# Half a pair as the unit of work through matmul, scaling and multiplication, in a kernel of 496 pairwise products

## The chip, the core and the metric

The kernel runs on one core of a Trainium2 chip. The metric is the device time of one execution in microseconds (us). Medians are quoted; all runs told of here were in the fast state, and executions of one kernel agree within about 0.5% (0.8% in e10). A profile's span is about 2 us shorter than the device time. Ratios are computed as the mean time of one kernel's runs over that of the other's of the same rounds, so they are not quite the ratio of the medians quoted.

Engines: PE is TensorE (PEld its weight loads), DVE VectorE, ACT ScalarE, POOL GpSimd, SP the engine that issues the transfers here.

## The reference, cut to what matters

```python
# r_inputs (1024, 32, 128) float32, W (496, 128, 128) float32; I_IDX, J_IDX: all pairs i < j of 32 fields
v_i = inputs[:, I_IDX, :]
v_j = inputs[:, J_IDX, :]
transformed = jnp.einsum('bpd,ped->bpe', v_i, W)
return transformed * v_j                          # (1024, 496, 128): 260 MB of output
```

## The kernel before

For each pair q the output is a tile of 128 x 1024 float32 (two PSUM banks). The first 15 pairs are multiplied directly. In the other 481 the matmul works on split operands: each weight and field is cut by ScalarE and POOL into h, l and d. Two products (h with h, l with l) accumulate in PSUM, ScalarE multiplies the sum in place by 1 + EPS, a third product (d with d) is added on top, VectorE multiplies with the other field into an output tile, and SP stores it.

I call the first two products F and the third S. Between F and S of the same pair the scaling must run, so the source puts the S of an older pair there: it stands LAG pairs behind.

```python
LAG = 2
wpool = ctx.enter_context(tc.tile_pool(name="ws", bufs=3))
opool = ctx.enter_context(tc.tile_pool(name="o", bufs=6))
ppool = ctx.enter_context(tc.tile_pool(name="ps", bufs=4, space=bass.MemoryType.PSUM))   # tiles of 1024: 2 banks each
# ...
for q in range(NQ + LAG):
    if q < NQ:
        # ... every 4 pairs: load the weights of chunk c+3, split those of c+2; per field: load and split
        po[q] = ppool.tile([P, BT], F32, tag="po", name=f"po_{q}")
        # ...
                for t in (0, 1):                                  # F: four matmuls of 512 columns
                    for h in range(0, BT, HB):
                        nc.tensor.matmul(po[q][:, h : h + HB], w_s[c][t][:, r], x_s[i][t][:, h : h + HB],
                                         start=t == 0, stop=t == 1)
                nc.scalar.mul(po[q], po[q], 1.0 + EPS)            # scaling
    if q >= LAG:
        if q - LAG >= nq0:
            second(q - LAG)                                       # S: two matmuls
        finish(q - LAG)                                           # multiplication and store
```

(Calls reflowed, cuts marked with dots.) The framework in which the kernel is written sets all waits itself, and when it compiles it may also put the instructions of an engine into another order than the source has.

## Time and profile before

| | before |
|---|---|
| median of the runs beside the changed kernel | 897.93 us (896.86 to 898.89) |
| profiled span | 896.0 us |
| TensorE busy / DMA share of 16 engines | 85% / 92.3% |
| S waits for the scaling (PEld + PE) | 162.8 + 123.0 us |

How to read the group lines that the prediction shows: busy us in total, mean ns of one, then the engine's idle time before them and what ended most of it. A wait line has the waiting engine, line and tile, what it waited for, us in total, how often, and the longest.

### The profile page before, as it was taken

The numbers are of one execution on the slowest core, as the hardware profiler recorded it, in microseconds if no ns is written. First come the engines' busy times: TensorE is split into PE (matmuls) and PEld (weight loads), VectorE is DVE, ScalarE is ACT, GpSimd is POOL, SyncE is SP. The second block draws the span as 40 slices with busy tenths as digits, with TensorE's granted clock in tenths as the row PEclk, the third lists the DMA queues.
The fourth block names the chain that finished last, engine by engine and source line by source line (L and its number), as shares of the span: only waits on it lengthen the run. The fifth ranks groups of instructions, "written<-read, shape, count | busy, mean of one in ns | idle before, by whom it ended". The sixth has DMA issues, their size and how long they took to land.

```text
span 896.0 us, 10407 instructions
## 1 busy us (share of the span) xinstructions
PE 761.1 (85%) x2946; PEld 526.2 (59%) x2946; DVE 607.0 (68%) x498; ACT 558.2 (62%) x655; POOL 549.5 (61%) x523
## 2 busy tenths in 40 slices
PE   7988888888888888888888888888888888898887
PEld 2455555555666565555565666655656566665665
DVE  3666666666777666676676767776667777677766
ACT  2266666666676566566665667665756666666565
POOL 1878877777666774664747565665655647474441
PEclk9999999999999999999999999999999999999999
DMA  8999999899999898998998999998998899999997
GB/s 329 416 340 370 360 355 343 318 361 338 376 357 362 332 370 327 339 361 320 353 343 336 343 363 356 355 352 321 355 341 334 336 339 330 343 345 339 337 342 304
DMA packets 94666, 310.03 MB, mean 346 GB/s; under 512 B 10513, under 2 KB 10769, under 8 KB 94609
## 3 DMA queue, kind: packets, MB, share of 16 engines
q1 hardware_dynamic: 94608, 309.37, 92.3%
q8 instruction: 23, 0.38, 0.2%
q14 instruction: 35, 0.28, 0.1%
HBM read 49.28 MB, written 260.05 MB: 345 GB/s over the span
## 4 chain that ended last, share of the span: by engine, by line
PE 32%; ACT 25%; issue 19%; POOL 11%; DMA 1%; DVE 0%; POOLq 0%; ACTq 0%; DVEq 0%
ACT po L177 20%; PE po L170 17%; PE po L135 14%; ACT wh L86 4%; POOL wl L87 4%; POOL wd L89 4%; POOL whs L88 2%; DMA out_dram<-ot 1%; ACT xh L100 1%; POOL xls L101 1%; DVE ot L128 0%; POOL xl L102 0%; POOLq L87 0%; ACTq L177 0%; POOL xd L103 0%
## 5 line engine op out<-in xcount | busy, mean ns | idle before, releaser
L128 DVE TENSOR_TENSOR ot<-po,x 128x1024 f32<-128x1024 f32 (+1 forms) x498 | 607.0, 1220 | 285.4 <-ACT po L177 141.7
L177 ACT ACTIVATE po<-po 128x1024 f32<-128x1024 f32 x481 | 476.9, 1009 | 298.5 <-PE po L170 298.5
L135 PE MATMUL po<-xd,wd 128*128 128x512 f32 x962 | 325.7, 420 | 123.8 <-ACT po L177 123.0
L87 POOL TENSOR_TENSOR wl<-w,wh 128x512 fp32r<-128x512 f32 x121 | 154.5, 1277 | 301.7 <-ACT wh L86 301.7
L135 PEld LDWEIGHTS po<-xd,wd 128*128 128x128 f32 x962 | 152.7, 188 | 257.5 <-ACT po L177 162.8
L170 PE MATMUL po<-xh,wh 128*128 128x512 f32 x962 | 300.9, 394 | 0.0
L170 PE MATMUL po<-xl,wl 128*128 128x512 f32 x962 | 298.1, 391 | 0.0
L170 PEld LDWEIGHTS po<-xl,wl 128*128 128x128 f32 x962 | 180.6, 188 | 42.2
L170 PEld LDWEIGHTS po<-xh,wh 128*128 128x128 f32 x962 | 180.6, 188 | 42.1 <-issue 0.5
L89 POOL TENSOR_TENSOR wd<-wl,whs 128x512 fp32r<-128x512 f32 x121 | 156.6, 1294 | 7.9
L86 ACT ACTIVATE wh<-w 128x512 fp32r<-128x512 f32 x121 | 75.5, 624 | 19.3 <-DMA w<-in_wt_dram 19.3
L88 POOL TENSOR_SCALAR whs<-wh 128x512 f32<-128x512 f32 x121 | 75.1, 621 | 10.2
L101 POOL TENSOR_TENSOR xls<-x,xh 128x512 f32<-128x512 f32 x52 | 67.4, 1296 | 4.2
L103 POOL TENSOR_TENSOR xd<-xh,xl 128x512 fp32r<-128x512 f32 x52 | 66.9, 1287 | 2.2
L100 ACT ACTIVATE xh<-x 128x512 fp32r<-128x512 f32 x52 | 32.1, 621 | 13.6 <-PE po L170 8.7
L102 POOL TENSOR_SCALAR xl<-xls 128x512 fp32r<-128x512 f32 x52 | 32.4, 623 | 4.4
L159 PE MATMUL po<-x,w 128*128 128x512 f32 x60 | 29.6, 656 | 6.2 <-DMA x<-in_xt_dram 6.2
L159 PEld LDWEIGHTS po<-x,w 128*128 128x128 f32 x60 | 12.3, 209 | 22.6 <-issue 21.6
L86 ACT ACT_TABLE_LOAD x1 | 1.3, 1283 | 0.7 <-PEq L196 0.7
L196 POOL MEMSET const-float32-0.0<- 128x1 f32 x1 | 0.1, 99 | 0.2 <-issue 0.2
L196 POOL MEMSET const-bfloat16-1.0<- 128x1 bf16 x1 | 0.1, 102 | 0.0
L196 POOL MEMSET const-uint8-127<- 128x1 uint8 x1 | 0.1, 102 | 0.0
(1 smaller groups left out, 0.1 us busy)
## 6 DMA issues: line engine op xcount, KB each, us to landing
out_dram<-ot SPq DMA_DIRECT2D x494, 512.0 KB, 3.8
w<-in_wt_dram SPq DMA_DIRECT2D x123, 256.0 KB, 3.9
x<-in_xt_dram SPq DMA_DIRECT2D x30, 512.0 KB, 6.0
x<-in_xt_dram SPq DMA_DIRECT2D x4, 256.0 KB, 4.4
out_dram<-ot SPq DMA_DIRECT2D x4, 256.0 KB, 2.6
w<-in_wt_dram SPq DMA_DIRECT2D x1, 192.0 KB, 2.6
w<-in_wt_dram SPq DMA_DIRECT2D x1, 64.0 KB, 1.8
```

Source lines behind the costliest of these rows:

```text
L86: nc.scalar.mul(h, raw, 1.0 - 2.0**-13)
L87: nc.gpsimd.tensor_tensor(l, raw, h.bitcast(F32), ALU.subtract)
L88: nc.gpsimd.tensor_scalar(hs, h.bitcast(F32), EPS, 1.0, ALU.mult, ALU.mult)
L89: nc.gpsimd.tensor_tensor(d, l.bitcast(F32), hs, ALU.subtract)
L100: nc.scalar.mul(h[:, s], x_sb[f][:, s], 1.0 - 2.0**-13)
L101: nc.gpsimd.tensor_tensor(ls, x_sb[f][:, s], h[:, s].bitcast(F32), ALU.subtract)
L103: nc.gpsimd.tensor_tensor(d[:, s], h[:, s].bitcast(F32), l[:, s].bitcast(F32), ALU.subtract)
L128: nc.vector.tensor_tensor(ot[:, s], po[q][:, s], x_sb[j][:, s], ALU.mult)
L135: nc.tensor.matmul(po[q][:, h : h + HB], w_s[q // WC][2][:, r], x_s[i][2][:, h : h + HB], start=False, stop=True, skip_group_check=True,)
L159: nc.tensor.matmul(po[q][:, h : h + HB], w_raw[c][:, q % WC, :], x_sb[i][:, h : h + HB], start=True, stop=True,)
L170: nc.tensor.matmul(po[q][:, h : h + HB], w_s[c][t][:, r], x_s[i][t][:, h : h + HB], start=t == 0, stop=t == 1,)
L177: nc.scalar.mul(po[q], po[q], 1.0 + EPS)
```

## The change

Its intent: a unit is half a pair, so that each PSUM bank goes round by itself. A unit's bank is scaled, finished and freed sooner, eight banks replace four pairs of banks, and S follows three units behind. The store is still one per pair. Loads of the first two fields are issued from ScalarE.

```diff
-LAG = 2
+LAG = 3
-    ppool = ctx.enter_context(tc.tile_pool(name="ps", bufs=4, space=bass.MemoryType.PSUM))
+    ppool = ctx.enter_context(tc.tile_pool(name="ps", bufs=8, space=bass.MemoryType.PSUM))
-    load_x(NF - 2, 2)
-    load_x(NF - 1, 2)
+    load_x(NF - 2, 2, nc.scalar)
+    load_x(NF - 1, 2, nc.scalar)
...
+    def first(u):
+        q, h = divmod(u, 2)
...
+        po[u] = ppool.tile([P, HB], F32, tag="po", name=f"po_{u}")
...
+            for t in (0, 1):
+                nc.tensor.matmul(po[u], w_s[c][t][:, r], x_s[i][t][:, s], start=t == 0, stop=t == 1)
+            nc.scalar.mul(po[u], po[u], 1.0 + EPS)
+
+    def second(u):
...
+            nc.tensor.matmul(
+                po[u], w_s[q // WC][2][:, r], x_s[i][2][:, s], start=False, stop=True, skip_group_check=True
+            )
...
+        nc.vector.tensor_tensor(ots[q][:, s], po.pop(u), x_sb[j][:, s], ALU.mult)
...
+    for u in range(2 * NQ + LAG):
...
+            first(u)
+        if u >= LAG:
+            second(u - LAG)
```

More of the change, by code (lines that the diff above doesn't have):

```diff
@@ L61, with load_x @@
     opool = ctx.enter_context(tc.tile_pool(name="o", bufs=6))
-    ppool = ctx.enter_context(tc.tile_pool(name="ps", bufs=4, space=bass.MemoryType.PSUM))
+    ppool = ctx.enter_context(tc.tile_pool(name="ps", bufs=8, space=bass.MemoryType.PSUM))
     x_sb = {}
-    def load_x(f, pieces=1):
+    def load_x(f, pieces=1, eng=None):
         x_sb[f] = xpool.tile([P, BT], F32, tag=f"x{f}", name=f"x_{f}")
@@ L69, in load_x @@
         for k in range(pieces):
-            nc.sync.dma_start(out=x_sb[f][:, k * s : (k + 1) * s], in_=xt[:, f, k * s : (k + 1) * s])
+            (eng or nc.sync).dma_start(out=x_sb[f][:, k * s : (k + 1) * s], in_=xt[:, f, k * s : (k + 1) * s])
     w_raw = {}
@@ L116 @@
     load_w(2)
-    out_v = out.rearrange("q e b -> q e b")
-    po = {}
-    def finish(q):
-        j = pairs[q][1]
-        ot = opool.tile([P, BT], F32, tag="ot", name=f"ot_{q}")
-        pieces = 2 if q >= NQ - 2 else 1
-        s0 = BT // pieces
-        for k in range(pieces):
-            s = slice(k * s0, (k + 1) * s0)
-            nc.vector.tensor_tensor(ot[:, s], po[q][:, s], x_sb[j][:, s], ALU.mult)
-            nc.sync.dma_start(out=out_v[q, :, s], in_=ot[:, s])
-    def second(q):
-        i, _ = pairs[q]
-        r = slice(q % WC * P, (q % WC + 1) * P)
-        for h in range(0, BT, HB):
+    po, ots = {}, {}
@@ new lines, in first @@
+    def first(u):
+        q, h = divmod(u, 2)
+        i, c = pairs[q][0], q // WC
+        r = slice(q % WC * P, (q % WC + 1) * P)
+        s = slice(h * HB, (h + 1) * HB)
+        po[u] = ppool.tile([P, HB], F32, tag="po", name=f"po_{u}")
+        if q < nq0:
+            nc.tensor.matmul(po[u], w_raw[c][:, q % WC, :], x_sb[i][:, s], start=True, stop=True)
+        else:
+            for t in (0, 1):
+                nc.tensor.matmul(po[u], w_s[c][t][:, r], x_s[i][t][:, s], start=t == 0, stop=t == 1)
+            nc.scalar.mul(po[u], po[u], 1.0 + EPS)
@@ L135, in second @@
+    def second(u):
+        q, h = divmod(u, 2)
+        i, j = pairs[q]
+        r = slice(q % WC * P, (q % WC + 1) * P)
+        s = slice(h * HB, (h + 1) * HB)
+        if q >= nq0:
             nc.tensor.matmul(
-                po[q][:, h : h + HB], w_s[q // WC][2][:, r], x_s[i][2][:, h : h + HB], start=False, stop=True,
-                skip_group_check=True,
-            )
-    for q in range(NQ + LAG):
-        if q < NQ:
+                po[u], w_s[q // WC][2][:, r], x_s[i][2][:, s], start=False, stop=True, skip_group_check=True
+            )
+        if h == 0:
+            ots[q] = opool.tile([P, BT], F32, tag="ot", name=f"ot_{q}")
+        nc.vector.tensor_tensor(ots[q][:, s], po.pop(u), x_sb[j][:, s], ALU.mult)
+        if q >= NQ - 2:
+            nc.sync.dma_start(out=out[q, :, s], in_=ots[q][:, s])
+        elif h == 1:
+            nc.sync.dma_start(out=out[q], in_=ots[q])
@@ L142 @@
+    for u in range(2 * NQ + LAG):
+        if u < 2 * NQ:
+            q = u // 2
             i, j = pairs[q]
             c = q // WC
-            if q % WC == 0:
+            if u % (2 * WC) == 0:
                 if c + 3 < nchunk:
                     load_w(c + 3)
-                for k in ([c + 2] if c > 0 else [0, 1, 2]):
+                for k in [c + 2] if c > 0 else [0, 1, 2]:
                     if c0 <= k < nchunk:
                         split_w(k)
-            if j == i + 1:
-                for f in ([i - 4] if i < NF - 2 else [NF - 6]):
-                    if f >= 0:
-                        load_x(f)
+            if u % 2 == 0 and j == i + 1:
+                f = i - 4 if i < NF - 2 else NF - 6
+                if f >= 0:
+                    load_x(f)
@@ L154 @@
                 if 0 <= i - 1 < NF - 1 - NATIVE:
                     split_x(i - 1)
-            po[q] = ppool.tile([P, BT], F32, tag="po", name=f"po_{q}")
-            if q < nq0:
-                for h in range(0, BT, HB):
-                    nc.tensor.matmul(
-                        po[q][:, h : h + HB],
-                        w_raw[c][:, q % WC, :],
-                        x_sb[i][:, h : h + HB],
-                        start=True,
-                        stop=True,
-                    )
-            else:
-                r = slice(q % WC * P, (q % WC + 1) * P)
-                for t in (0, 1):
-                    for h in range(0, BT, HB):
-                        nc.tensor.matmul(
-                            po[q][:, h : h + HB],
-                            w_s[c][t][:, r],
-                            x_s[i][t][:, h : h + HB],
-                            start=t == 0,
-                            stop=t == 1,
-                        )
-                nc.scalar.mul(po[q], po[q], 1.0 + EPS)
@@ L178 @@
-        if q >= LAG:
-            if q - LAG >= nq0:
-                second(q - LAG)
-            finish(q - LAG)
+            first(u)
+        if u >= LAG:
+            second(u - LAG)
 def kernel(**inputs):
```

## The prediction

> **What bounds the kernel now.** I read the page first (busy shares, DMA queue, groups), then the waits, then the order of TensorE's work in the middle of the run, then DMA over short windows.
>
> ```profile
> PE 761.1 (85%) x2946; PEld 526.2 (59%) x2946; DVE 607.0 (68%) x498; ACT 558.2 (62%) x655; POOL 549.5 (61%) x523
> DMA packets 94666, 310.03 MB, mean 346 GB/s; under 512 B 10513, under 2 KB 10769, under 8 KB 94609
> q1 hardware_dynamic: 94608, 309.37, 92.3%
> L128 DVE TENSOR_TENSOR ot<-po,x 128x1024 f32<-128x1024 f32 (+1 forms) x498 | 607.0, 1220 | 285.4 <-ACT po L177 141.7
> L177 ACT ACTIVATE po<-po 128x1024 f32<-128x1024 f32 x481 | 476.9, 1009 | 298.5 <-PE po L170 298.5
> ```
>
> No vector engine is near full: DVE, ACT and POOL each lie idle about a third of the time. TensorE shows 85%, but that is modelled. The DMA engines show 92% at a mean of 346 GB/s. So two candidates remain: TensorE with gaps, and the DMA. The waits say where TensorE stops:
>
> ```profile
> PEld po L135 <- ACT po L177: 162.8, 195, 1.7
> DVE ot L128 <- ACT po L177: 141.7, 89, 1.6
> PE po L135 <- ACT po L177: 123.0, 245, 1.2
> ```
>
> The third product (L135) waits 245 times for ScalarE's scaling (L177). Nothing waits for an output transfer here, so the DMA isn't a wait yet. In TensorE's own order of time (start us, length, count, idle before):
>
> ```profile
> 455.58 0.73 PE L135 MATMUL po<-xd,wd 128*128 128x512 f32 x2 [0.69 <-ACT po L177]
> 456.14 0.63 PE L170 MATMUL po<-xh,wh 128*128 128x512 f32 x2
> ...
> 457.07 0.62 PE L170 MATMUL po<-xh,wh 128*128 128x512 f32 x2
> 457.53 0.61 PE L170 MATMUL po<-xl,wl 128*128 128x512 f32 x2
> 458.43 0.70 PE L135 MATMUL po<-xd,wd 128*128 128x512 f32 x2 [0.28 <-ACT po L177]
> 458.96 0.63 PE L170 MATMUL po<-xh,wh 128*128 128x512 f32 x2
> ...
> 459.89 0.62 PE L135 MATMUL po<-xd,wd 128*128 128x512 f32 x2
> 460.35 0.62 PE L170 MATMUL po<-xh,wh 128*128 128x512 f32 x2
> ...
> 461.27 0.63 PE L135 MATMUL po<-xd,wd 128*128 128x512 f32 x2
> 462.60 0.73 PE L135 MATMUL po<-xd,wd 128*128 128x512 f32 x2 [0.69 <-ACT po L177]
> ```
>
> Call the first two products of a pair F (four matmuls) and the third S (two). The source says F S F S with S two pairs behind. What stands here is S, F F S F S F S, S: two S and two F adjoin, and S follows its own F by one pair, or by none (the S at 462.60 belongs to the F at 460.35). The program was reordered when it was compiled. Undisturbed, S plus F takes 461.27 - 459.89 = 1.38 us. Four pairs take 462.60 - 455.58 = 7.02 us instead of 4 x 1.38 = 5.52. The lost 1.50 us: 0.44 before 458.43, 0.87 before 462.60 (1.33 instead of 0.46), the rest in S pairs that start 0.1 us slower. Over 481 pairs, 481/4 x 1.50 = 180 us. **TensorE's gaps behind the scaling are the bound**, and the DMA stands close behind:
>
> ```profile
> 24.00:28.00 4.00, 4.00 (x11) 1.80 (x10) 3.02 (x3) 0.00 (x0) 3.76 (x5) 1.00 1.04 420
> 28.00:32.00 4.00, 4.00 (x11) 1.81 (x10) 2.93 (x3) 0.63 (x1) 3.83 (x5) 1.00 1.02 416
> 440.00:445.00 5.00, 3.62 (x15) 2.37 (x15) 2.06 (x2) 2.77 (x3) 2.77 (x3) 1.00 0.99 376
> 445.00:450.00 5.00, 4.28 (x19) 3.15 (x18) 4.29 (x4) 2.62 (x4) 2.16 (x3) 1.00 0.72 266
> 450.00:455.00 5.00, 4.61 (x19) 3.06 (x18) 3.07 (x4) 3.86 (x5) 1.34 (x2) 1.00 0.85 329
> ```
>
> The last two columns are DMA share and GB/s. Fed without a break (the first 40 us) the engines move 416 to 422 GB/s; in the middle they get 266 to 376, because outputs arrive unevenly. So the 92% isn't saturation[...].
>
> **What the Trainium skill says.** "PSUM — Partial Sum Buffer", Terms and "The four PSUM rules": a matmul's output lies in one bank of 512 float32, there are eight, and two engines may not be in one bank at once. A pair of 1024 columns is two banks, so four pair buffers are all of PSUM and so are eight half buffers; the change adds no memory, it frees each bank sooner. "Perfetto Trace Analysis", "Identifying Performance Opportunities": a consistent bubble can mean too few buffers for the next tile; the pattern that repeats every four pairs agrees. The same page, "Optimizing Scalar/DVE Operations": an instruction on PSUM carries about 51 ns on ScalarE and 125 ns on VectorE, and profiled latency hides an overlap. The trace: two scalings back to back last 1.93 us though one lasts 1.01, so the pitch is 0.92; the four half-wide multiplications at the end last 685 ns each, two of them 1.29 together, a pitch of 0.61. "DMA: Bandwidth & Descriptors", "Issuing engines are not separate DMA queues": another issuing engine saves issue time only; no run before shows loads from ScalarE.
>
> **The change part by part.**
> 1. TensorE: same matmuls, same weight loads (2946 each): 481 x 1.38 = 664 us, with no gain or loss from the halves.
> 2. ScalarE: 962 scalings of 512 instead of 481 of 1024. A half's pitch is an estimate, half of 0.92 plus half the skill's 51 ns, 0.49 us; 962 x 0.49 = 471 instead of 481 x 0.92 = 443. With 173 splits at about 0.53: 563 us. It costs 28 us, beside other work.
> 3. VectorE: 992 halves at 0.61 to 0.685 are 605 to 680 us instead of 607. Its pitch per pair, 1.22 to 1.37, stays just under TensorE's 1.38. Not on the path, but with little left.
> 4. The PSUM loop, in source order. Before: F 0.92, two further S and F 2.76, S 0.46, handover 0.2, multiplication 1.22: 5.56 us until the bank is free, against the 5.52 in which four buffers come round. No slack, so any split of 0.62 us on ScalarE breaks the order into what we saw. After: F 0.46, three units 2.07, S 0.23, handover 0.2, multiplication 0.69: 3.65 against the same 5.52, so 1.87 us of slack. This is the gain.
> 5. The lag: between an F and its S now lie 3 x 0.69 = 2.07 us; handover 0.2 plus a scaling of about 0.6 plus a split of 0.54 ahead of it is 1.34. It fits. So the 180 us can go: 896 - 180 = 716 us if TensorE alone set the end.
> 6. Loads of the first two fields from ScalarE: TensorE waits 6.2 us for x before 9.91 us. They share bandwidth with the loads they now overlap, so I count 1 us of gain.
> 7. DMA: same bytes, 310.03 MB. At 1.38 us per pair the store alone is 0.524 MB / 1.38 = 380 GB/s, the weights 0.262 MB per four pairs another 47, the fields about 17 MB over 664 us another 20 (with the first ones, which came earlier): near 445, above the 416 to 422 that it reached. So **the DMA becomes the bound before TensorE does**. Floor: 310.03 MB / 0.416 = 745 us, plus about 4 us of start and tail: 749. Over the whole run in windows of 4 us, the 44 windows with a DMA share of at least 1.02 moved 403 GB/s on average: 310.03 / 0.403 = 769, plus 4: 773. I add 7 us for the early fields, where POOL's split of a field (two halves of 1.30 + 0.62 + 1.29 us, 6.4 us) comes every 6 to 10 pairs, and for leftover gaps: 780. The runs' median lies 2 us above the profiled span, hence **782 us**.
>
> **The rivals.**
> (a) The order stays broken. The new order is also made when compiling, and it broke before at the start of each group of four pairs, where the split weights come due. If what broke it is POOL or ScalarE and not PSUM, TensorE still drains there: one scaling of 0.6 us and handovers, about 0.9 us per four pairs, 120 x 0.9 = 108 us over 715: 820 to 830. For it: the alignment with the four pairs. Against: POOL is 61% busy and waits 302 us for the weights' first split.
> (b) TensorE's floor is reached because stores pack better than I think: 716 to 745. Against: no stretch above 422 GB/s.
> (c) VectorE becomes the bound. If a half costs its full 685 ns plus the 0.16 us seen between multiplications, 0.845 x 992 = 838 us, about 850 in all. Against: that 0.16 is TensorE's pace showing, since queued halves took 0.61.
> (d) The saturated DMA with mostly stores does only 360, as some windows at full share did (356 at a share of 1.0): 861 us and no gain over 5%. Against: the stretches over 410 directly after a backlog.
>
> **Range and chances.** The central case is DMA at 403 GB/s; its floor at 416 gives 749, and with an even flow perhaps 752. Upwards (a), and parts of (c) and (d), reach 820 to 850. Range 752 to 835. Within 2% means above 880, which needs (d) or a badly broken order together with more; slower needs a new stall bigger than the old.
>
> **What would show it.** Right: L135's waits for L177 fall from 123 us to below 30; TensorE shows source order; the mean rate rises to about 395 GB/s, with most slices over 390; VectorE, or the output's issue, now waits for landed outputs. Step 2 is checked by the scaling's mean (near 580 ns), step 3 by 685 ns. Wrong: L135 still waiting for scalings by the hundred (a); VectorE above 90% (c); DMA share at 1.0 with 360 GB/s (d); a rate above 425 (b).

## The result, and the profile after

The changed kernel takes **931.2 us** (930.87 to 931.59, 4 runs) against 897.93: ratio 1.0371, 95% interval 1.0353 to 1.0389. It is slower; the range of the prediction ended at 835.

From the page of the changed kernel: busy shares, what the DMA moved, the two groups.

```profile
PE 856.3 (92%) x2946; PEld 500.4 (54%) x2946; DVE 676.1 (73%) x992; ACT 628.8 (68%) x1136; POOL 549.3 (59%) x523
DMA packets 94676, 310.12 MB, mean 334 GB/s; under 512 B 10512, under 2 KB 10768, under 8 KB 94608
L145 DVE TENSOR_TENSOR ot<-po,x 128x512 f32<-128x512 f32 x992 | 676.1, 691 | 250.4 <-PE po L140 230.1
L132 ACT ACTIVATE po<-po 128x512 f32<-128x512 f32 x962 | 548.6, 582 | 273.9 <-PE po L131 245.9
```

TensorE's 92% instead of 85% isn't more work: in the order of time below a matmul is recorded as 0.39 us long though the next begins 0.23 us after it (458.62, 458.85), so a stop of up to 0.16 us leaves no gap in the record. Weight loads, of which there are as many as before, went from 526.2 to 500.4 us busy. The DMA is less used than before (334 against 346 GB/s). The waits of the third product, now line 140, for the scaling, now line 132:

```profile
PEld po L140 <- ACT po L132: 263.0, 703, 1.0
ACT po L132 <- PE po L131: 245.9, 355, 5.3
PE po L140 <- ACT po L132: 42.6, 146, 0.6
```

The prediction wanted 123 us to fall below 30. Both kinds together went from 285.8 us in 440 waits to 305.6 us in 849. TensorE's order of time shows where (F is lines L131, S is L140; start us, length, count):

```profile
456.44 0.47 PE L140 MATMUL po<-xd,wd 128*128 128x512 f32 x1 [0.30 <-ACT po L132]
...
458.05 0.50 PE L140 MATMUL po<-xd,wd 128*128 128x512 f32 x1
458.38 0.40 PE L131 MATMUL po<-xh,wh 128*128 128x512 f32 x1
458.62 0.39 PE L131 MATMUL po<-xl,wl 128*128 128x512 f32 x1
458.85 0.39 PE L140 MATMUL po<-xd,wd 128*128 128x512 f32 x1
...
459.69 0.49 PE L140 MATMUL po<-xd,wd 128*128 128x512 f32 x1
...
461.41 1.10 PE L140 MATMUL po<-xd,wd 128*128 128x512 f32 x2
462.35 0.39 PE L131 MATMUL po<-xh,wh 128*128 128x512 f32 x1
...
463.74 0.47 PE L140 MATMUL po<-xd,wd 128*128 128x512 f32 x1 [0.30 <-ACT po L132]
```

The same pattern as before stands here, with halves: F F S F S F S ... S S over eight units, then again. From 456.44 to 463.74 are 7.30 us for four pairs; before it was 7.02. Over 120 such groups that is 0.28 x 120 = 34 us, less 2.9 us that the start gained (the first split product begins at 32.3 us instead of 35.2): 31, and the spans differ by 33.5. So the loss is in the pattern, all along the run (7.30 and 7.02 are also the medians over all groups of the two traces).

Is the lag of three units there? The listing of the compiled program gives each engine's instructions in their final order. This is TensorE's in the changed kernel; the number after po is the unit (48 rows per eight pairs, cut):

```
L131 Matmult po_488 <- xh, wh_61     L131 Matmult po_488 <- xl, wl_61
L131 Matmult po_489 <- xh, wh_61     L131 Matmult po_489 <- xl, wl_61
L140 Matmult po_488 <- xd, wd_61
L131 Matmult po_490 <- xh, wh_61     L131 Matmult po_490 <- xl, wl_61
L140 Matmult po_489 <- xd, wd_61
...
L140 Matmult po_494 <- xd, wd_61
L140 Matmult po_495 <- xd, wd_61
L131 Matmult po_496 <- xh, wh_62     (the next group of four pairs)
```

It isn't. S(488) stands one unit behind F(488), and S(495) directly behind S(494), with no F after its own. Counted over each compiled program, how many F start between an F and its S:

| program | LAG in the source | 0 | 1 | 2 | 3 |
|---|---|---|---|---|---|
| before (pairs) | 2 | 125 | 356 | 0 | |
| changed (halves) | 3 | 130 | 828 | 1 | 3 |
| changed, LAG 1 (built, not run) | 1 | 131 | 826 | 5 | 0 |
| changed, LAG 5 (built, not run) | 5 | 130 | 830 | 1 | 1 |

Counted from the order of TensorE's instructions in the traces, the first two rows come out the same. The lag in the source made next to no difference to the compiled program. A lag of one *pair* had become a lag of one *half*.

### The profile page after: what moved, and what is told of

It reads as the page before. It is cut to its first block, busy times and chain, and to the rows that moved or that the text cites. A ratio compares the mean times of both kernels' runs of the same rounds, so it can differ in the third digit from the quotient of the medians.

```text
span 929.5 us, 11870 instructions
## 1 busy us (share of the span) xinstructions
PE 856.3 (92%) x2946; PEld 500.4 (54%) x2946; DVE 676.1 (73%) x992; ACT 628.8 (68%) x1136; POOL 549.3 (59%) x523
## 2 busy tenths in 40 slices
DMA packets 94676, 310.12 MB, mean 334 GB/s; under 512 B 10512, under 2 KB 10768, under 8 KB 94608
## 4 chain that ended last, share of the span: by engine, by line
PE 58%; ACT 16%; POOL 15%; issue 8%; DMA 2%; DVE 0%; POOLq 0%; SPq 0%; ACTq 0%; DVEq 0%
PE po L131 30%; PE po L140 26%; ACT po L132 14%; POOL xls L101 5%; POOL xd L103 4%; POOL wd L89 2%; POOL xl L102 2%; DMA out_dram<-ot 2%; PE po L128 2%; POOL wl L87 1%; POOL whs L88 1%; ACT xh L100 1%; ACT wh L86 1%; DVE ot L145 0%; DMA x<-in_xt_dram 0%
## 5 line engine op out<-in xcount | busy, mean ns | idle before, releaser
L145 DVE TENSOR_TENSOR ot<-po,x 128x512 f32<-128x512 f32 x992 | 676.1, 691 | 250.4 <-PE po L140 230.1
L132 ACT ACTIVATE po<-po 128x512 f32<-128x512 f32 x962 | 548.6, 582 | 273.9 <-PE po L131 245.9
L140 PE MATMUL po<-xd,wd 128*128 128x512 f32 x962 | 440.1, 458 | 65.5 <-ACT po L132 42.6
L131 PE MATMUL po<-xl,wl 128*128 128x512 f32 x962 | 379.6, 395 | 0.0
L131 PE MATMUL po<-xh,wh 128*128 128x512 f32 x962 | 379.2, 394 | 0.0
L140 PEld LDWEIGHTS po<-xd,wd 128*128 128x128 f32 x962 | 179.2, 186 | 351.3 <-ACT po L132 263.0
L131 PEld LDWEIGHTS po<-xl,wl 128*128 128x128 f32 x962 | 180.5, 188 | 41.9 <-POOL wl L87 0.2
L131 PEld LDWEIGHTS po<-xh,wh 128*128 128x128 f32 x962 | 181.3, 189 | 11.8 <-issue 0.2
L102 POOL TENSOR_SCALAR xl<-xls 128x512 fp32r<-128x512 f32 x52 | 32.3, 622 | 4.4
```

Of the source, the lines that this page charges most:

```text
L102: nc.gpsimd.tensor_scalar(l[:, s], ls, 1.0 / EPS, 1.0, ALU.mult, ALU.mult)
L131: nc.tensor.matmul(po[u], w_s[c][t][:, r], x_s[i][t][:, s], start=t == 0, stop=t == 1)
L132: nc.scalar.mul(po[u], po[u], 1.0 + EPS)
L140: nc.tensor.matmul(po[u], w_s[q // WC][2][:, r], x_s[i][2][:, s], start=False, stop=True, skip_group_check=True)
L145: nc.vector.tensor_tensor(ots[q][:, s], po.pop(u), x_sb[j][:, s], ALU.mult)
```

## The experiments

Theory 1: the compiled order took the lag away, and TensorE stops behind the scaling as before, only twice as often. Theory 2: halves cost more in themselves (fixed parts of the doubled instructions on ScalarE and VectorE, twice the handovers). A third question was the prediction's: where the DMA binds.

The first tool is a call of the framework that pins an instruction behind the one that stands before it on the same engine in the source. It adds no wait for completion.

### e1, e2, e3, e4

e1 and e2, the change and the kernel before with TensorE held in source order (all matmul calls alike):

```diff
-                nc.tensor.matmul(po[u], w_s[c][t][:, r], x_s[i][t][:, s], start=t == 0, stop=t == 1)
+                tc.keep_in_program_order(nc.tensor.matmul(po[u], w_s[c][t][:, r], x_s[i][t][:, s], start=t == 0, stop=t == 1))
```

> The changed kernel with TensorE's matmuls held in source order, so that the third product stands three units behind in the compiled program too (in the changed kernel as compiled it stands one unit behind in 828 of 962 cases and none in 130). Theory 1 (the compiled order took the lag away, TensorE stops behind the scaling): the waits of the third product for the scaling fall from about 306 us together to under 40, and the time falls from 931 to 760 to 810, where the output transfers bind. Theory 2 (halves cost more in themselves: fixed parts of the doubled number of instructions on ScalarE and VectorE and twice the handovers): stays above 890.

> The kernel before, whole pairs, with TensorE's matmuls held in source order (third product two pairs behind; compiled as it was, one behind in 356 of 481 cases and none in 125). Theory 1: faster as well, 770 to 830; if the four pair buffers are as tight as the prediction says (5.56 us against 5.52), it lies 10 to 40 us above e1. Theory 2: about 20 us under e1 or more, and both near their unheld times (898 and 931).

e3 is e1 with a lag of one:

```diff
-LAG = 3
+LAG = 1
```

> As e1 with a lag of one unit in the source. Theory 1: between an F and its S lies 0.69 us (one S, one F) where the handovers and a half's scaling need about 0.86, so each unit takes about 0.82 instead of 0.69: 962 x 0.82 = 789, plus 41 of start and end: 830 to 850; the rest up to 931 is then the emptying at each group of four pairs. Theory 2: near 931.

e4 is the changed kernel, not held, with half the bytes stored:

```diff
-            nc.sync.dma_start(out=out[q], in_=ots[q])
+            nc.sync.dma_start(out=out[q, :, :HB], in_=ots[q][:, :HB])
```

> The changed kernel with only the first half of each output stored (wrong result on purpose, 130 MB less; the compiled order then is the source's, three units behind in 959 of 962 cases, without being held). Theory 1: the transfers are out of the way, TensorE alone sets the end: 700 to 730. Theory 2: above 850, since the halves' costs are all still there.

Measured (ratios to the kernel before in the same rounds):

| run | what | lag compiled | us | ratio (95%) |
|---|---|---|---|---|
| e1 | halves, held | 3 | 776.88 | 0.866 (0.865 to 0.868) |
| e2 | pairs, held | 2 | 781.46 | 0.871 (0.870 to 0.873) |
| e3 | halves, held, LAG 1 | 1 | 860.73 | 0.960 (0.958 to 0.962) |
| e4 | halves, half of each output stored (wrong result) | 3 | 712.57 | 0.795 (0.793 to 0.796) |

Theory 1 holds: the same instructions in source order take 777 instead of 931, and the kernel before gains as well, 781 instead of 898. It is TensorE's order that differs: ScalarE's weight split stands behind the sixth scaling of a group both in the changed kernel's trace and in e1's, all 121 times. Theory 2 falls: e1 has all of the halves' costs, and its list has one wait of an S for the scaling, of 0.4 us. One expectation was missed: e2 lies 5 us above e1, not 10 to 40. So with the order held, the change itself is worth 0.6%. Lines of e1's page and waits:

```profile
PE 726.2 (94%) x2946; PEld 542.3 (70%) x2946; DVE 638.2 (82%) x992; ACT 624.1 (81%) x1136; POOL 549.7 (71%) x523
DMA packets 94676, 310.12 MB, mean 400 GB/s; under 512 B 10512, under 2 KB 10768, under 8 KB 94608
PEld po L131 <- DVE ot L145: 86.5, 137, 1.9
DVE ot L145 <- DMA out_dram<-ot: 41.0, 51, 1.9
```

Here the rate is 400 GB/s over the whole span, VectorE waits for output tiles still on their way to memory, and TensorE's F in turn waits for VectorE. The transfers bind e1, as the prediction had expected of the change.

e3 separates two parts of the loss. With a lag of one throughout and no emptying at each group it takes 861, and its S wait for the scaling again:

```profile
PEld po L140 <- ACT po L132: 206.4, 657, 0.6
```

Against e4's 713, where TensorE alone sets the end, that is 148 us over 962 units, 0.154 us each. I had expected 830 to 850: 0.82 us per unit was a little low. The rest, 931 - 861 = 70 us or 0.58 per group of four pairs, I put down to the emptying. That is not shown by itself: in e3 ScalarE's weight split stands behind the last scaling of a group and not behind the sixth, and e9 below shows that its place alone can be worth 26 us.

The lag's arithmetic can be read from the changed kernel's order of time above: the second matmul of an F begins at 458.62 and the next instruction could begin at 458.85; its S begins at 459.69. These 0.84 us are the scaling (0.58) with its handovers (0.26). A lag of one half covers S and F of halves, 0.69 us, so the S at 459.69 stops for 0.15; the next instruction starts another 0.1 late, and these 0.25 us let the next S pass without a stop. So every second S stops: 458.05 to 459.69 are 1.64 us for two units where two undisturbed ones take 1.38. Before, with a lag of one pair, the S at 458.43 belongs to the F at 456.14, which is through at 457.07: the scaling (1.01) and its handovers (0.35) took 1.36 us, and S and F of a pair cover 1.38. The cover was halved by the change; the thing to be covered wasn't.

### e5, e6, e7, e8: pairs against halves, and how much lag

e5 is e2 with half of each output stored:

```diff
-            nc.sync.dma_start(out=out_v[q, :, s], in_=ot[:, s])
+            nc.sync.dma_start(out=out_v[q, :, k * s0 : k * s0 + s0 // 2], in_=ot[:, k * s0 : k * s0 + s0 // 2])
```

> As e2 (whole pairs, TensorE in source order), with half of each output stored (wrong result on purpose). It asks what the halves are worth when the transfers are out of the way; e4, the same with halves, took 713. If the four pair buffers bind (in e2 the weight loads of F wait 432 times for the multiplication, 134 us): a pair stays at about 1.50 us, 481 x 1.50 + 41 = 763, so 750 to 775. If in e2 the transfers were the bound and the buffers only passed that on: 710 to 725.

e6 is e2 with LAG = 1; e7 and e8 are e1 with LAG = 2 and LAG = 5.

> As e2 with a lag of one pair in the source. Between an F and its S then lie S and F of whole pairs, 1.39 us, where the scaling with its handovers needs about 1.26: only the pairs with a split of 0.54 us ahead stop, about 0.4 us per four pairs, 49 us over a TensorE floor of 705, so the transfers still bind: 770 to 790, while the same lag of one with halves (e3) took 861. If a lag of one hurts whole pairs as it hurts halves: 840 to 870.

> As e1 with a lag of two units: 1.39 us between an F and its S against about 0.86 needed, 1.40 with a split ahead. Theory 1: nothing left to wait for, 772 to 785, as e1 (777). If the lag matters in proportion to its number: halfway to e3, about 815.

> As e1 with a lag of five units. The way round a bank grows by two units to 3.65 + 1.38 = 5.03 us against 5.52, still inside. If the transfers bind: 772 to 785 again. If the looser lag helps further: under 765; if the banks become tight: over 790.

| run | what | us | ratio (95%) |
|---|---|---|---|
| e5 | pairs, held, LAG 2, half of each output stored (wrong result) | 778.75 | 0.868 (0.867 to 0.870) |
| e6 | pairs, held, LAG 1 | 781.13 | 0.871 (0.869 to 0.873) |
| e7 | halves, held, LAG 2 | 778.69 | 0.869 (0.866 to 0.871) |
| e8 | halves, held, LAG 5 | 777.68 | 0.867 (0.865 to 0.869) |

e5 shows what the change set out to cure. With 130 MB less to store, pairs stay at 779 (expected 750 to 775 if the buffers bind, so 4 us over) while halves (e4) reach 713. The wait line of e5, and its order of time:

```profile
PEld po L170 <- DVE ot L128: 137.5, 429, 2.3
```

```profile
456.95 0.73 PE L170 MATMUL po<-xh,wh 128*128 128x512 f32 x2
...
459.99 0.73 PE L170 MATMUL po<-xh,wh 128*128 128x512 f32 x2
...
463.02 0.73 PE L170 MATMUL po<-xh,wh 128*128 128x512 f32 x2
```

F waits for the multiplication that frees its buffer, 429 times, once for nearly every pair. The F at 463.02 takes the buffer of the one at 456.95, four pairs earlier: 6.07 us for four pairs, 1.52 each. So four pair buffers at a lag of two hold TensorE at 1.52 us per pair where it could do 1.38, and eight halves at a lag of three lift that: 66 us, but only where neither the order nor the transfers are in the way. How much of the 66 us needs halves is open, because e4 also has the shorter lag (three halves are 2.07 us, two pairs 2.76). e2's 781 comes from this round of the buffers (its same wait is 134.1 us, 432 times), e1's 777 from the transfers; that they come out so near to each other is chance.

e6 shows that a lag of one doesn't hurt pairs: 781, where it costs halves 861. The shorter lag also shortens the round of the buffers (that wait falls to 41.1 us, 80 times), and the transfers bind at 398 GB/s. Between its waits for the transfers e6 runs at 1.38 us per pair (S begin at 457.53, 458.90, 460.28 and 461.67), where e5's pairs take 1.38 and 1.65 in turn, so a shorter lag is a rival to halves here; pairs at a lag of one with half of each output stored were not run. e7 and e8 show that with halves a lag of two or five does as well as three: 1.38 us of cover is enough for 0.84.

### e9 to e12: is there a part of the transfers in it, and a better version

e9 is e3 with half of each output stored (the diff of e4). e10 gives each half its own output tile and store:

```diff
-    opool = ctx.enter_context(tc.tile_pool(name="o", bufs=6))
+    opool = ctx.enter_context(tc.tile_pool(name="o", bufs=12))
...
+        ot = opool.tile([P, HB], F32, tag="ot", name=f"ot_{u}")
+        nc.vector.tensor_tensor(ot, po.pop(u), x_sb[j][:, s], ALU.mult)
+        nc.sync.dma_start(out=out[q, :, s], in_=ot)
```

> As e3 (halves, held in source order, a lag of one unit: 861), with half of each output stored (wrong result on purpose). If TensorE's stop behind the scaling is all that binds at this lag: 845 to 862. If the transfers had a part in e3's time, as the drop from e1 to e4 (777 to 713) might suggest: under 820.

> As e1 with an output tile and a store for each half (12 tiles of 512 instead of 6 of 1024; the same bytes, rows of 2 KB instead of 4 KB). An attempt at a better version: e1 moves 400 GB/s on average and its VectorE waits 41 us for output tiles. If finer tiles keep the transfers better fed: 755 to 770. If the engines' rate is all there is: 774 to 785; if shorter rows cost rate: over 790.

e9 took 887.08 us (ratio 0.989), *more* than e3, and missed both of its expectations. In its compiled program ScalarE's weight split stands one unit earlier, ahead of the last scaling of a group instead of behind it; ScalarE had not been held. e11 and e12 hold it too, with full and with half stores:

```diff
-        nc.scalar.mul(h, raw, 1.0 - 2.0**-13)
+        tc.keep_in_program_order(nc.scalar.mul(h, raw, 1.0 - 2.0**-13))
```

(and likewise the field's split and the scaling).

> e3 again (halves, a lag of one unit, full stores), now with ScalarE's instructions in source order too. e9 came out 26 us slower than e3 although it stores half, and in its compiled program ScalarE's splits stand at other places. With both held, e11 and e12 have the same order on both engines. If TensorE's stop behind ScalarE is all that binds at this lag: e11 and e12 within 10 us of each other, both between 850 and 900.

> e9 again with ScalarE's instructions in source order too: within 10 us of e11 if the transfers have no part at a lag of one; 25 us or more above e11 (as e9 over e3) if e9's delay came from something else than ScalarE's order; 25 us or more below if the transfers do bind in e11.

e11 took 861.18 us (0.961), e12 858.42 (0.958). So at a lag of one the transfers have next to no part, and e9's 26 us came with ScalarE's order. The changed kernel as compiled moves 334 GB/s, fewer than e11's 361, so I take the transfers to be out of its loss as well, though no run stored half in exactly its order.

e10 took 824.49 us (0.920), worse than e1's 777, as the last of its expectations had it. Its page (with a granted TensorE clock of 0.974, and a DMA share of 101.7%):

```profile
DMA packets 165823, 310.24 MB, mean 378 GB/s; under 512 B 18416, under 2 KB 18672, under 8 KB 165744
```

The same bytes in 165,823 packets instead of 94,676 moved at 378 instead of 400 GB/s. There are also twice as many stores, so whether the shorter rows or their number cost it is not separated. e1, the change with TensorE held in source order, is the fastest: correct, and 13.4% less time than the kernel before. e7 and e8 are equal to it within the noise, and pairs held in order (e2, e6) come within 1%.

### What moved the order

Compiling again with less stored, and counting as above (built; of these only the first and the last row were run, as the changed kernel and e4, and their traces give the same counts):

| stored of each output | 0 | 1 | 2 | 3 |
|---|---|---|---|---|
| all | 130 | 828 | 1 | 3 |
| 7/8 | 123 | 777 | 55 | 7 |
| 3/4 | 27 | 541 | 291 | 103 |
| 5/8 | 1 | 1 | 1 | 959 |
| 1/2 | 1 | 1 | 1 | 959 |

So the size of the stores enters into the order that the compile step gives to TensorE. The likely reading is that it orders by when it believes things will be ready, and that in its estimate the stores hold back the output tiles, these the multiplications, and these the PSUM banks, so that an F seems to have no bank yet and an older S, already scaled, is put ahead of it. That reading is argued: I did not look into the estimate. That the store's size moves the order, and that the order makes 154 us (931 to 777), is shown.

## Why the prediction was wrong

Point by point, by its own steps:

- **The bound before** (gaps of TensorE behind the scaling, 180 us) was right. Holding the source order removes the S's waits for the scaling, and the span falls by 118 us (e2) to where the round of the buffers or the transfers stop it.
- **Step 5 failed.** It said that between an F and its S "now lie 3 x 0.69 = 2.07 us". That holds for the source. In the compiled program the lag was one unit, 0.69 us, in 828 of 962 cases, and none in 130. The prediction had itself read from the trace before that the compiled order isn't the source's, and then reckoned both steps 4 and 5 in source order. In its place stood a stop of 0.154 us per unit on average (e3 against e4), and an emptying per group.
- **Rival (a)**, "the order stays broken", is what happened, but was sized at the emptying alone (820 to 830) and was not made the central case. The one-unit lag between the emptyings was missed; it costs 148 us (e3 against e4), and the emptying, with ScalarE's split at another place, the other 70.
- **Step 4**, the round of a PSUM buffer, is a limit that exists (e5), but it wasn't what had disturbed the order, as the prediction claimed: halves have the slack and the order broke all the same. The trace before already spoke against it: in its list of waits the bubble is one of S for the scaling, and no F waits for VectorE, so no wait for a PSUM buffer shows, though the prediction took the pattern of four pairs to agree with too few buffers. Its size was short too: 5.56 us estimated, 6.07 in e5. The F-to-S part took 4.07 instead of 3.68, since within one round other F stop as well.
- **Step 7 and the central case**: "DMA at 403 GB/s ... 780", 782 with the offset. With the order held, e1 moves 400 GB/s and takes 777. The reckoning was right for TensorE in source order, which the changed kernel as compiled was not.
- **Steps 2 and 3**: a scaling of a half lasts 582 ns ("near 580"), two queued ones 1.07 us together in the changed kernel's trace, a pitch of 0.49 us as estimated, and a multiplication 691 ns ("685"); neither engine bound, so rival (c) is out, with VectorE at 73%. Rival (d), a saturated DMA at only 360 GB/s, is refuted by e1's mean of 400. Rival (b), 716 to 745, was not reached with full stores; e4's 713 is the floor without them, close to the 716 of step 5.
- **Step 6** counted 1 us. The first split product began 2.9 us earlier, but in the other runs with the same loads it begins anywhere from 31.7 to 34.0 us, and in the runs of pairs from 33.9 to 37.0, and no run changed the loads alone: a gain of this size is not shown.

## What to carry to other kernels

Where a compiler orders the instructions, a software pipeline in the source is a wish: before sizing a change of the lag, count the lag in the compiled program, and if it isn't there, hold the order first. Here this is worth 116 to 154 us with no other edit, while the change of the unit alone cost 33, and with the order held gained 5 (781 to 777). When a unit of work is cut in half, the work that covers a dependency halves, but the handovers and fixed parts in it don't (1.36 us became 0.84, not 0.68), so a lag counted in units has to grow. And once two limits lie close together, as the round of the buffers and the transfers here, take one away to see the other.

## What the Trainium skill lacked or had wrong

- No page of the skill tells that a lag in the source may be gone in the compiled program. 898 became 781 us by order alone (e2), 931 became 777 (e1).
- "Perfetto Trace Analysis", "Optimizing Scalar/DVE Operations", says that breaking up instructions that cause bubbles may let work complete sooner. It lacks the other side for an engine that isn't saturated: the scaling with its handovers fell only from 1.36 to 0.84 us when halved, and at a lag of one unit the kernel was slower for it (e3, 861, against e6, 781).
- The same section puts the fixed part of an instruction on PSUM at about 51 ns on ScalarE and 125 ns on VectorE, and the profiled latency at about twice that. From the mean durations of halves and wholes, 2 x 582 - 1009 = 155 ns on ScalarE and 2 x 691 - 1220 = 162 ns on VectorE: more than twice 51 on the one, clearly less than twice 125 on the other.
- "Perfetto Trace Analysis", "Matmul Optimizations", advises to use all eight PSUM banks. Both kernels do; what counted was how long one buffer is held. Eight single banks at a lag of three against four pairs of them at a lag of two made 779 into 713 us once order and transfers were out of the way (e5, e4).
- "Perfetto Trace Analysis", "DMA Optimizations", says that going from 2 KB to 4 KB can improve throughput dramatically. In a saturated stream of stores it was 378 against 400 GB/s (e10, e1), with half as many stores besides.
